# Layer 1's softmax in five later pieces: how the subtraction, the exponential and their maxima are placed among the score groups of an attention layer

## The chip, the core and the metric

The kernel runs on one core of a Trainium2 chip. The core has a matrix engine (PE, with its weight loads shown apart as PEld), a vector engine (DVE), a scalar engine (ACT), a general engine (POOL) and SyncE (SP), which issues most transfers. Each engine works through its own queue in order. Matrix results land in PSUM, a small memory that is cut into tiles here; everything else lies in SBUF or in device memory. The metric is the time of one execution in device microseconds; the kernel before took 3659.3 us, the median of three runs from 3655.91 to 3659.39.

## The reference

Four layers follow one another on a tensor of 4 images, 64 x 64 pixels and 128 channels, all in float32: layer 0 is neighbourhood attention with a gate, layer 1 is full attention over an image, layer 2 a gated mix with a layer norm, layer 3 a selective state-space scan. The change is in layer 1:

```python
N = H * W                                    # 4096
h = group_norm(x, gn_scale, gn_bias)
hf = h.reshape(B, N, C)
q = hf @ wq + bq
k = hf @ wk + bk
v = hf @ wv + bv
w_ = jnp.einsum('bqd,bkd->bqk', q, k) * C ** (-0.5)
w_ = jax.nn.softmax(w_, axis=2)
o = jnp.einsum('bqk,bkd->bqd', w_, v)
o = o @ wo + bo
return x + o.reshape(B, H, W, C)
```

Every pixel of an image attends to all 4096 pixels of it, so each image has a score matrix of 4096 x 4096.

## The kernel before

The images are worked on one after the other: layer 0 of an image, then its layer 1. While layer 1 runs, short tasks of other layers are put between its steps by a function `between(i)`: layer 2 of the same image (`turn`, `mix`, `add`, `norm`: transposes, products into PSUM tiles `pr`, `pg`, `pl`, `py`, layer-norm statistics) and the front of layer 3 (`front`: projections `pi` and `pz`, copies `xh`, a depthwise convolution whose taps are DVE, ACT and POOL work on `acc`, `tp` and `gsum`, and the products `pd`). The rest of layer 3 runs after the last image.

Layer 1 takes the queries in 16 blocks of 256 and the keys in 16 groups of 256 (two tiles of 128). Scores are held with keys on the partitions and queries along the free dimension, so that exponentials can serve directly as the stationary operand of the product with the values. One step `s` of the loop is one score group; `i, g = divmod(s, 16)` are its block and group. A step holds:

- `score` (L638 to L644): two products into one of four PSUM tiles `sc` (512 wide), a copy by ACT into `st` (L642), and a running maximum over groups by DVE into `mx` (L644). The tile is free again when copy and maximum have been made. After group 15, `fold` (L647) takes the maximum of the two halves of `mx`.
- At group 1 of the next block `turn_maxima` (L652 to L657): `mx` is transposed by PE (`pt`), a reduction by DVE gives each query's negated maximum `nm`, queries on the partitions, and two multiplications put it on the diagonal of a 128 x 256 tile `dm` (two identity matrices scaled by `nm`).
- At group 2 `soften` (L661 to L665): the product of a matrix of ones with `dm` spreads the negated maxima over all partitions into a PSUM tile `pb`; then, in four parts of four groups (2048 wide), DVE adds `pb` to `st` and ACT takes the exponential.
- `value` (L674): seven steps after that block's last score group, the groups of exponentials are multiplied into `po`, four products of 129 columns per group; column 128 of the values is one, so it yields the sum of the exponentials. Group `gv` of block `j` is due at step 16 (j + 1) + 7 + gv. After the last group `finish` divides by the sum (`ri`, L680) and adds the result to the image.

The exponentials of 24 groups have room in `st` (three buffers of eight groups). The PSUM tiles are handed out in turn from three pools: four tiles `s` for scores and for most products of the between-tasks, two tiles `t` for transposes, `pt`, `pb` and `pd`, two tiles `o` for `po`.

The order in which the loop writes these steps is not the order on the engines: when the program is built, a scheduler sets each engine's order by its own costs, except where an instruction is kept in program order. So the score groups and value groups of PE stand partly alternately and partly in runs.

ACT computes each kind of function with a table, and a change of kind needs a table load, a row of its own in the trace (ACT_TABLE_LOAD). Exponential, copy, identity and tanh need no change among each other here; Silu (L843) and Sqrt (L762) do.

The steps of the loop and where the between-tasks come in:

```python
if 0 < i <= NB and g == 1:
    turn_maxima(blocks[i - 1])
if 0 < i <= NB and g == 2:
    soften(i - 1, blocks[i - 1])
...
t = s // 8
if (s % 8 == 7 or s == ng * (NB + 1) + LAG - 1) and t > 0:
    between(t - 1)
```

So `between(0)` comes at step 15, the last group of the first block, and then one task at every eighth step. In the first image `between(0)` is empty; in the others it projects two chunks of the image before (four `pi`) and begins their convolution.

Of the kernel before, what the change touches and what calls it, by code (L numbers as in the profile page):

```python
# [23 lines left out]
AF = mybir.ActivationFunctionType  # L24
ALU = mybir.AluOpType
# [4 lines left out]
P = 128  # L30
# [108 lines left out]
def layers_0_to_2(  # L139
    ctx, tc, xf, mata, matb, rows, rpb, convw, sel, ident, cl, dram, big, ring, early, x3_d, ub_d, zf_d, y_d, dbl_d, ct_d, gw_d, bw_d  # L140
):
    nc = tc.nc
# [10 lines left out]
    def ps_t(shape, name):  # L153
        return psp.tile(shape, F32, name=name, tag="t", bufs=2)
# [31 lines left out]
    def load_x(b, xt=None, tiles=(0, NT), queue=nc.sync, kept=False):  # L186
        if xt is None:
            xt = ring([P, NT, C], f"x_{b}")
        src = xf[b].rearrange("(r w) c -> r w c", w=W)
        for j in range(*tiles):  # L190
            r, c = BR * (j // 4), BC * (j % 4)
            ins = queue.dma_start(xt[:, j, :], src[r:r + BR, c:c + BC, :])
            if kept:

                tc.keep_in_program_order(ins)
        return xt
# [19 lines left out]
    for cv, n in enumerate(cols_of):  # L216
        t = t_d[cv].rearrange("q h d k -> (q h) (d k)")
# [45 lines left out]
    ones = wp.tile([P, P], F32, name="ones")  # L263
# [64 lines left out]
    def edge_bias(rv):  # L328

        t = wp.tile([P, HEADS * 11 * 60], F32, name="be", tag="be")  # L330
        if rv in edge_d:
            nc.sync.dma_start(t, edge_d[rv])
        else:
            nc.gpsimd.memset(t, NEG)
            a = 0
            for cv in range(3):
                n = HEADS * 11 * cols_of[cv]
                fill_bias(t[:, a:a + n], rv, cv, 0 if rv == 0 else H - BR)
                a += n
            edge_d[rv] = dram.tile([P, HEADS * 11 * 60], F32, name=f"edge_d{rv}")  # L340
            nc.sync.dma_start(edge_d[rv], t)
        return t

    def bias_tiles():
        return [wp.tile([P, HEADS * 14 * n], F32, name=f"bias_m{k}", tag=f"bm{k}") for k, n in enumerate(cols_of)]
# [231 lines left out]
    def layer_1(b, xt, hT, st, between):  # L577
# [44 lines left out]
        QB, G, LAG, NB = 2 * P, 2, 7, L // (2 * P)  # L622
        ng = NT // G
# [5 lines left out]
        def group(s, n=1):  # L629
            r, at = divmod(s % (3 * 8), 8)  # L630
            return rings[r][:, G * at:G * (at + n), :]

        def score(i, k, g):
            if g == 0:
                k.mx = tmp.tile([P, G, QB], F32, name="mx1", tag="mx1")
            ps = ps_s([P, G, QB], "sc1")
            for r in range(G):
                nc.tensor.matmul(  # L638
                    ps[:, r, :], lhsT=kT[:, bass.ts(G * g + r, P)], rhs=qT[:, bass.ts(i, QB)], start=True, stop=True
                )  # L640
            st = group(ng * i + g)
            nc.scalar.copy(st, ps)  # L642
            if g > 0:
                nc.vector.tensor_tensor(k.mx, group(ng * i) if g == 1 else k.mx, ps, ALU.max)  # L644

        def fold(k):
            nc.vector.tensor_tensor(k.mx[:, 0, :], k.mx[:, 0, :], k.mx[:, 1, :], ALU.max)  # L647

        def turn_maxima(k):
            pt = ps_t([P, 2, P], "pt1")  # L650
            for h in range(2):
                nc.tensor.transpose(pt[:, h, :], k.mx[:, 0, bass.ts(h, P)], ident)  # L652
            nm = sml.tile([P, 2], F32, name="nm1", tag="nm1")
            nc.vector.tensor_reduce(nm, pt, AX.X, ALU.max, negate=True)
            k.dm = tmp.tile([P, 2, P], F32, name="dm1", tag="dm1", bufs=1)
            for h in range(2):
                nc.vector.tensor_scalar(k.dm[:, h, :], ident, nm[:, h:h + 1], None, ALU.mult)  # L657

        def soften(i, k):
            pb = ps_t([P, QB], "pb1")  # L660
            nc.tensor.matmul(pb, lhsT=ones, rhs=k.dm.rearrange("p h q -> p (h q)"), start=True, stop=True)  # L661
            for g in range(0, ng, 4):
                part = group(ng * i + g, 4)
                nc.vector.tensor_tensor(part, part, pb.unsqueeze(1).to_broadcast([P, 4 * G, QB]), ALU.add)  # L664
                nc.scalar.activation(part, part, AF.Exp)  # L665

        def value(i, k, g):
            if g == 0:
                k.po = ps_o([P, 2, C + 1], "po1")
            st = group(ng * i + g)  # L670
            for r in range(G):
                j = G * g + r
                for h in range(2):
                    nc.tensor.matmul(  # L674
                        k.po[:, h, :], lhsT=st[:, r, bass.ts(h, P)], rhs=v[:, j, :], start=(j == 0 and h == 0), stop=(j == NT - 1 and h == 1)
                    )

        def finish(i, k):
            ri = sml.tile([P, 2], F32, name="ri1", tag="ri1")
            nc.vector.reciprocal(ri, k.po[:, :, C])  # L680
            for h in range(2):
                x = xt[:, 2 * i + h, :]
                nc.vector.scalar_tensor_tensor(x, k.po[:, h, 0:C], ri[:, h:h + 1], x, ALU.mult, ALU.add)

        blocks = {}
        for s in range(ng * (NB + 1) + LAG):
            i, g = divmod(s, ng)
            if i < NB:
                k = blocks.setdefault(i, Block())
                score(i, k, g)  # L690
                if g == ng - 1:
                    fold(k)
            if 0 < i <= NB and g == 1:
                turn_maxima(blocks[i - 1])
            if 0 < i <= NB and g == 2:
                soften(i - 1, blocks[i - 1])
            j, gv = divmod(s - ng - LAG, ng)
            if j >= 0:
                value(j, blocks[j], gv)
                if gv == ng - 1:  # L700
                    finish(j, blocks.pop(j))
            t = s // 8
            if (s % 8 == 7 or s == ng * (NB + 1) + LAG - 1) and t > 0:
                between(t - 1)


# [440 lines left out]
    for b in range(B):  # L1147
# [8 lines left out]
        def between(i):  # L1156

            n, part = divmod(i - 6, 4)
            if i == 6 and b + 1 < B:
                ahead.append(load_x(b + 1))  # L1160
            if i >= 6 and n < NCH:
                parts[part](n)
            first_part(i)
            if b + 1 < B and i == NT + 1:
                edge_of[b + 1] = edge_bias(0)
            if b + 1 < B and i == NT + 3:
                bias_m[:] = bias_tiles()
                for t, d in zip(bias_m, bias_d):
                    nc.sync.dma_start(t, d)

        first_part = front(b)
        first_part(-1)
        layer_1(b, xt, *handed.pop(b), between)
        if b + 1 < B:
            coming = layer_0(b + 1, ahead[0], edge_of[b + 1])
# [385 lines left out]
```

## Time and profile before

| what | us |
|---|---|
| median of three runs | 3659.3 |
| the profiled execution | 3657.49 |
| its span on the engines | 3655.7 |
| layer 1, images 1 to 4, with the tasks between | 198 to 747, 918 to 1483, 1654 to 2218, 2388 to 2958 |
| layer 0 of images 1 to 4 | 0 to 198, 747 to 918, 1483 to 1654, 2218 to 2388 |
| layer 3's scans and output | about 3020 to 3656 |
| a score matmul start to start, a step's score group | 0.22, 0.87 |
| a value group of a step | 0.89 |
| addition of `pb`, 128 x 2048 (DVE, L664) | 2.28 |
| exponential, 128 x 2048 (ACT, L665) | 1.91 |
| score copy (ACT, L642) and maximum (DVE, L644), 128 x 512 | 0.59 and 0.69 |
| table load (ACT), 237 of them | 1.28 |

How to read it: PE shows two records for one float32 product, so a score group is four records and a value group eight. The idle time of a row is that of its engine just before it, and behind the arrow stands what ended it. In a windows line the numbers are the stretch, its length, the busy time of PE, PEld, DVE, ACT and POOL (with the number of instructions), the granted clock of PE as a share of full speed, the share of the transfer engines and GB/s.

### The profile page before, as it was taken

What the parts mean: (1) busy time and instruction counts of PE and PEld (TensorE: products, weight loads), DVE (VectorE), ACT (ScalarE), POOL (GpSimd) and SP (SyncE); (2) the same over time, 40 slices, a digit from 0 to 9 for tenths busy, and PEclk for the clock granted to TensorE, in tenths of its full rate; (3) what the DMA queues carried; (4) which work ended last, traced back from release to release, by engine and by line L of the source; (5) the groups of instructions that cost most, each with busy time, mean ns of one, the idle gap of its engine ahead of it and who ended that gap; (6) DMA issues with size and microseconds to landing.
All of it is one profiled execution on the core that took longest, in us unless ns stands there. A gap on an engine that the chain in (4) does not pass through costs nothing. (4 is left out here: it accounts for less than half of the span.)

```text
span 3655.7 us, 61448 instructions
## 1 busy us (share of the span) xinstructions
PE 3293.8 (90%) x22234; PEld 2603.0 (71%) x22234; DVE 2773.2 (76%) x5070; ACT 2619.3 (72%) x4324; POOL 1416.7 (39%) x1592
## 2 busy tenths in 40 slices
PE   7999999999999999998999999989999987666647
PEld 4679988866788888666888886668888852222246
DVE  5757777767768777677787776767877768999968
ACT  4855667778667777686676777866767759999934
POOL 6500012245112222451122224521222338999856
PEclk8999999999999999999999999999999995555579
DMA  4200000131001012410021213100100279999998
GB/s 123 73 25 3 12 18 27 54 100 35 24 27 45 27 45 87 135 39 24 24 79 30 77 54 101 40 1 24 45 30 34 69 225 211 214 238 217 201 275 284
DMA packets 189362, 310.38 MB, mean 85 GB/s; under 512 B 23007, under 2 KB 111996, under 8 KB 184156
## 3 DMA queue, kind: packets, MB, share of 16 engines
q1 hardware_dynamic: 146260, 220.27, 18.0%
q0 software_dynamic: 24384, 76.95, 11.9%
q10 hardware_dynamic: 18416, 9.24, 0.9%
q8 instruction: 176, 2.88, 0.3%
q14 instruction: 126, 1.03, 0.1%
HBM read 167.69 MB, written 155.56 MB: 88 GB/s over the span
## 5 line engine op out<-in xcount | busy, mean ns | idle before, releaser
L674 PEld LDWEIGHTS po<-v,st 128*128 128x128 f32 x8192 | 1049.2, 193 | 73.5 <-issue 35.7
L674 PE MATMUL po<-v,st 128*128 128x129 f32 x8192 | 1067.8, 277 | 17.6 <-ACT st L665 17.6
L638 PE MATMUL sc<-qT,kT 128*128 128x256 f32 x4096 | 1025.7, 382 | 12.7 <-DVE mx L644 12.5
L642 ACT COPY st<-sc 128x512 f32<-128x512 f32 x1024 | 580.5, 587 | 454.2 <-PE sc L638 452.6
L644 DVE TENSOR_TENSOR mx<-mx,sc 128x512 f32<-128x512 f32 x896 | 613.2, 684 | 275.7 <-ACT st L642 252.3
L638 PEld LDWEIGHTS sc<-qT,kT 128*128 128x128 f32 x4096 | 718.9, 191 | 105.7 <-issue 13.9
L664 DVE TENSOR_TENSOR st<-st,pb 128x2048 f32<-128x2048 f32 x256 | 572.4, 2280 | 29.0 <-PE pb L661 28.7
L665 ACT ACTIVATE st<-st 128x2048 f32<-128x2048 f32 x256 | 484.6, 1910 | 28.5 <-DVE st L664 27.2
L1271 PE MATMUL pdt<-dbl,dt 8*128 8x512 f32 x512 | 307.5, 1081 | 142.3 <-ACT de L1278 141.7
L1282 POOL TENSOR_TENSOR inp<-de,ub 128x1024 f32<-128x1024 f32 x128 | 409.6, 4391 | 6.8 <-ACT de L1278 6.3
L1271 PEld LDWEIGHTS pdt<-dbl,dt 8*128 8x128 f32 x512 | 114.2, 312 | 332.8 <-ACT de L1278 270.0
L505 POOL TENSOR_SCALAR pr<-pr,sm 128x308 f32<-128x308 f32 (+3 forms) x512 | 243.9, 496 | 205.1 <-DVE sm L503 186.8
L746 POOL TENSOR_TENSOR x<-x,row 128x512 f32<-128x512 f32 x32 | 47.9, 1498 | 707.1 <-DVE mx L644 686.7
L892 POOL TENSOR_TENSOR gsum<-gsum,tp 128x504 f32<-128x504 f32 (+1 forms) x177 | 229.2, 1301 | 127.1 <-ACT gsum L880 73.8
L497 ACT ACTIVATE pr<-pr,mx 128x308 f32<-128x308 f32 (+3 forms) x512 | 262.8, 517 | 1.3 <-DVE mx L486 1.3
L1309 DVE TENSOR_TENSOR_SCAN h<-h,end,inp 128x1024 f32<-128x1024 f32 x96 | 221.1, 2346 | 20.3 <-ACT h L1295 9.7
L514 PE MATMUL pt<-ident,pr 128*88 128x128 f32 (+5 forms) x1472 | 205.4, 276 | 9.8 <-ACT prT L516 8.8
L901 DVE SCALAR_TENSOR_TENSOR acc<-xh,cc,acc 128x512 f32<-128x512 f32 (+3 forms) x250 | 199.5, 803 | 10.2 <-ACT acc L865 8.6
L1324 POOL DMA_DIRECT2D y<-yo x112 | 200.6, 2710 | 13.1 <-DMA y<-y 4.8
L742 POOL TENSOR_TENSOR o<-o,rt 128x512 f32<-128x512 f32 x32 | 34.3, 1070 | 438.9 <-DVE o L741 434.4
L514 PEld LDWEIGHTS pt<-ident,pr 128*88 128x88 f32 (+5 forms) x1472 | 164.6, 138 | 45.2 <-ACT prT L516 25.9
L483 DVE CUSTOM_DVE_ANT_0 pr<-sc,bias_m 128x266 f32<-128x266 f32 (+1 forms) x384 | 152.1, 452 | 56.7 <-PE sc L479 55.1
(235 smaller groups left out, 4964.8 us busy)
## 6 DMA issues: line engine op xcount, KB each, us to landing
y<-yo POOLq DMA_DIRECT2D x112, 512.0 KB, 10.4
y<-y SPq DMA_DIRECT2D x48, 512.0 KB
zf_d<-zf SPq DMA_DIRECT2D x64, 256.0 KB
ub_d<-u SPq DMA_DIRECT2D x64, 256.0 KB
ub<-ub_d SPq DMA_DIRECT2D x16, 1024.0 KB
yl<-y SPq DMA_DIRECT2D x64, 256.0 KB
zc<-zf_d SPq DMA_DIRECT2D x64, 256.0 KB
v_d<-vg SPq DMA_DIRECT2D x128, 64.0 KB
```

The source lines that it names most:

```text
L497: pin(nc.scalar.activation(k.pr[:, h], k.pr[:, h], AF.Exp, bias=k.mx[:, h:h + 1], accum_out=k.sm[:, h:h + 1]))
L505: nc.gpsimd.tensor_scalar(k.pr[:, h], k.pr[:, h], k.sm[:, h:h + 1], 1.0, ALU.mult, ALU.mult)
L514: pin(nc.tensor.transpose(pt[0:n, h, :], k.pr[:, h, at:at + n], ident))
L638: nc.tensor.matmul(ps[:, r, :], lhsT=kT[:, bass.ts(G * g + r, P)], rhs=qT[:, bass.ts(i, QB)], start=True, stop=True)
L642: nc.scalar.copy(st, ps)
L644: nc.vector.tensor_tensor(k.mx, group(ng * i) if g == 1 else k.mx, ps, ALU.max)
L664: nc.vector.tensor_tensor(part, part, pb.unsqueeze(1).to_broadcast([P, 4 * G, QB]), ALU.add)
L665: nc.scalar.activation(part, part, AF.Exp)
L674: nc.tensor.matmul(k.po[:, h, :], lhsT=st[:, r, bass.ts(h, P)], rhs=v[:, j, :], start=(j == 0 and h == 0), stop=(j == NT - 1 and h == 1))
L892: nc.gpsimd.tensor_tensor(a, a, p, ALU.add)
L1271: nc.tensor.matmul(pdt[j][:, g, :], lhsT=dt[o:o + RANK, P * f:P * f + P], rhs=at(dbl[o:o + RANK, :], k & 2, g0, g0 + CH), start=True, stop ...
L1282: nc.gpsimd.tensor_tensor(by_rows(inp), by_rows(de), at(ub_s[f], b ^ (k & 1), SC * n, SC * n + SC), ALU.mult)
```

## The change

Three things are rewritten, and the computation stays the same. The two multiplications for the diagonal become one tensor_tensor of the identity and the negated maxima, both broadcast. The product with ones moves from group 2 to group 3 (`spread`). The subtraction and the exponential are no longer made in one go of four parts but in five parts at groups 3, 4, 5, 7 and 9, the first two of them two groups wide (1024) and the others four. Besides, the first task between the steps, `between(0)`, moves from step 15 to step 20, group 4 of the second block; all other tasks stay.

```diff
             k.dm = tmp.tile([P, 2, P], F32, name="dm1", tag="dm1", bufs=1)
-            for h in range(2):
-                nc.vector.tensor_scalar(k.dm[:, h, :], ident, nm[:, h:h + 1], None, ALU.mult)
-
-        def soften(i, k):
-            pb = ps_t([P, QB], "pb1")
-            nc.tensor.matmul(pb, lhsT=ones, rhs=k.dm.rearrange("p h q -> p (h q)"), start=True, stop=True)
-            for g in range(0, ng, 4):
-                part = group(ng * i + g, 4)
-                nc.vector.tensor_tensor(part, part, pb.unsqueeze(1).to_broadcast([P, 4 * G, QB]), ALU.add)
-                nc.scalar.activation(part, part, AF.Exp)
+            nc.vector.tensor_tensor(
+                k.dm, ident.unsqueeze(1).to_broadcast([P, 2, P]), nm.unsqueeze(2).to_broadcast([P, 2, P]), ALU.mult
+            )
+
+        def spread(k):
+            k.pb = ps_t([P, QB], "pb1")
+            nc.tensor.matmul(k.pb, lhsT=ones, rhs=k.dm.rearrange("p h q -> p (h q)"), start=True, stop=True)
+
+        softened = {3: (0, 2), 4: (2, 2), 5: (4, 4), 7: (8, 4), 9: (12, 4)}
+
+        def soften(i, k, g, n):
+            part = group(ng * i + g, n)
+            nc.vector.tensor_tensor(part, part, k.pb.unsqueeze(1).to_broadcast([P, n * G, QB]), ALU.add)
+            nc.scalar.activation(part, part, AF.Exp)
...
-            if 0 < i <= NB and g == 2:
-                soften(i - 1, blocks[i - 1])
+            if 0 < i <= NB and g == 3:
+                spread(blocks[i - 1])
+            if 0 < i <= NB and g in softened:
+                soften(i - 1, blocks[i - 1], *softened[g])
...
             t = s // 8
-            if (s % 8 == 7 or s == ng * (NB + 1) + LAG - 1) and t > 0:
+            if s == ng + 4:
+                between(0)
+            elif (s % 8 == 7 or s == ng * (NB + 1) + LAG - 1) and t > 1:
                 between(t - 1)
```

## The prediction

> **What bounds the kernel now.** I read the page's busy shares and slices first, then the stages by windows, then the idle time of TensorE by group inside layer 1, and last the timeline at one place. The page:
>
> ```profile
> PE 3293.8 (90%) x22234; PEld 2603.0 (71%) x22234; DVE 2773.2 (76%) x5070; ACT 2619.3 (72%) x4324; POOL 1416.7 (39%) x1592
> ...
> PE   7999999999999999998999999989999987666647
> ...
> PEclk8999999999999999999999999999999995555579
> ...
> L664 DVE TENSOR_TENSOR st<-st,pb 128x2048 f32<-128x2048 f32 x256 | 572.4, 2280 | 29.0 <-PE pb L661 28.7
> L665 ACT ACTIVATE st<-st 128x2048 f32<-128x2048 f32 x256 | 484.6, 1910 | 28.5 <-DVE st L664 27.2
> ```
>
> TensorE is full in the first 33 slices; layer 3 behind them is another regime, which the change doesn't touch. Layer 1 of the four images, from first score to last value product (window, its length, then busy PE, PEld, DVE, ACT, POOL, then the granted clock):
>
> ```profile
> 221.80:747.00 525.20, 512.40 (x3382) 463.44 (x3381) 398.57 (x575) 345.33 (x442) 68.84 (x59) 0.99 0.08 26
> 941.30:1483.00 541.70, 527.62 (x3475) 467.88 (x3474) 417.12 (x603) 389.74 (x519) 126.62 (x112) 0.99 0.15 45
> 1678.00:2218.00 540.00, 525.87 (x3467) 466.11 (x3466) 418.37 (x603) 389.30 (x518) 128.38 (x113) 0.99 0.17 52
> 2412.00:2957.20 545.20, 532.09 (x3478) 468.55 (x3477) 423.44 (x611) 399.86 (x536) 145.81 (x136) 0.99 0.14 44
> ```
>
> PE is busy 98%; it idles 12.8, 14.1, 14.1 and 13.1 us, 54.1 in all. DVE has over 120 us to spare per image and ACT over 140. The 54.1 us are the ceiling, with what the clock loses after an idle stretch. All of the idle time stands before three groups (second image):
>
> ```profile
> L674 PE MATMUL po<-v,st 128*128 128x129 f32 x2048 | 266.6, 276 | 4.8 <-ACT st L665 4.8
> L638 PE MATMUL sc<-qT,kT 128*128 128x256 f32 x1024 | 257.0, 382 | 3.3 <-DVE mx L644 3.2
> ...
> L661 PE MATMUL pb<-dm,ones 128*128 128x256 f32 x32 | 10.5, 409 | 6.0 <-DVE dm L657 5.3 <-DVE rd L763 0.4
> ```
>
> In the same view images 1, 3 and 4 give 3.1, 4.8, 4.8 (po), 4.0, 3.3, 2.1 (sc) and 5.6, 6.0, 6.1 (pb). Sums over four images: po 17.5, sc 12.7, pb 23.7. The timeline where the second image's first values begin:
>
> ```profile
> 965.21 0.70 PE L661 MATMUL pb<-dm,ones 128*128 128x256 f32 x2 [1.52 <-DVE dm L657]
> 965.75 1.89 PE L638 MATMUL sc<-qT,kT 128*128 128x256 f32 x8
> 972.46 4.64 PE L674 MATMUL po<-v,st 128*128 128x129 f32 x20 [4.83 <-ACT st L665]
> ...
> 966.74 8.87 DVE L664 TENSOR_TENSOR st<-st,pb 128x2048 f32<-128x2048 f32 x4
> ...
> 969.12 1.28 ACT L665 ACT_TABLE_LOAD   x1
> 970.41 7.31 ACT L665 ACTIVATE st<-st 128x2048 f32<-128x2048 f32 x4
> ```
>
> PE runs out of scores and waits for a whole 2048-wide subtraction and exponential. DVE takes no maximum for 8.87 us, so the score buffers stay full. Then the clock falls:
>
> ```profile
> 972.40:978.40 6.00, 5.94 (x24) 5.70 (x25) 5.79 (x7) 5.32 (x3) 0.29 (x1) 0.50 0.00 0
> ```
>
> 6 us at 0.50 lose 3.0 us. The same windows at the other starts: 1705.5 to 1712.3 and 2439.4 to 2446.2 at 0.50 with 4.5 and 4.8 us of work (2.25 and 2.4 lost), 247.4 to 252 at 0.63 (1.7 lost); and twice in mid-image 1, 504 to 507.4 and 562 to 565.4 at 0.50 (1.7 each). Together 12.75, so the ceiling is 54.1 + 12.75 = 66.9 us.
>
> **Part by part.** A step is one score group (0.87 us of PE by the starts) and one value group (0.89), 1.76 us.
>
> *Five parts; layer 2/3 work moved at the start.* From the 512-wide maximum (686 ns) and the 2048-wide addition (2280) I interpolate 1.22 us for a 1024-wide addition; a 1024-wide activation takes 1.06 (u, L843). So the first values can begin 2.28 + 1.91 - 1.22 - 1.06 = 1.9 us sooner after pb. In images 2 to 4 `between(0)` also moves (in image 1 it is empty). It issues no DMA; with it POOL's row copies and ACT's first convolution products come five steps later, 3 steps ahead of the next task, which needs them. Its four projections `pi`, which stood before pt, now stand around pb, by the order of the built program: scores 0 to 4, one pi, pb, three pi, score 5, po. Counted from the last score of block 1, pb stands at five groups x 0.87 + pt 0.22 + one pi 0.86 = 5.4; then PE has pb 0.5, three pi 2.6 and a score group 0.9, and wants po at 9.4. ACT evicts the first pi (to 6.2), does acc 0.81, tp 0.72, the load 1.28 and the half-size exponential 1.06: 10.1. PE waits 0.7 instead of 4.83, and pb doesn't wait. Now gone: po 17.5, the pb waits there (1.52, 1.52, 1.17 = 4.2) and the half clock behind (9.35), 31.0. I leave 1.0 per image for this wait and scores that wait for pi's buffers: 27.0 saved. Bounds: 8 (1.9 x 4) and 31. I take near the upper, since what fills the gap are products that have to run anyway.
>
> *pb a group later.* Between pt and pb stood one step of PE work, 1.76 us, in nearly all blocks; in the built program it is 3.3 to 3.5. The other pb waits, 23.7 - 4.2 = 19.5, are at most 2.5 long, one such per image; 1.76 more cover leaves about 0.65 x 4 = 2.6: 16.9 saved, bounds 0 and 19.5. What is queued behind the longer-held result: pb keeps one of two "t" buffers until the fifth addition, at about group 10; the next products that need that buffer come with the tasks of group 15, so nothing waits. New is that the fourth addition stands on DVE behind ri, which waits for the last value product of the block before (group 6); its values are wanted at group 15, and behind it only maxima could be late.
>
> *The diagonal by one product.* Two of 0.28 become one 256-wide tensor_tensor; the nearest row is the fold, 424 ns. -0.1 to +0.15 us, off the path with 1.76 us of new cover: 0. It no longer has a maximum between its halves, which in the 2.5 us waits stood waiting for a score copy.
>
> *Bursts broken up.* Additions stand three in a row (6.67 us) or four between two maxima; in the built program mostly one, at worst a 1024 and a 2048 (3.4, eased by four score buffers x 1.76 us). Of sc's 12.7 I leave 3.0, and the two half-clock stretches of image 1 go (3.4), since the 2.0 and 2.5 us waits ahead of them do: 13.1 saved, bounds 0 and 16.1.
>
> *What is added.* Per block one addition (2 x 1.22 - 2.28 = 0.16) and one exponential (2 x 1.06 - 1.91 = 0.21); and with exponentials spread over groups 3 to 9, other tables come between: 266 loads stand in ACT's order instead of 237. 29 x 1.28 = 37 us plus 64 x 0.21 = 13: 50 us of ACT, 13 per image, against 140 us spare. Nothing on the path if scores are copied in time. Where a part with its load stands between two copies of even blocks, ACT goes 6.7 us without a copy (sg, o 0.69 each, exponential 1.91, load 1.28, zf 1.08, u 1.06) against 4.8 before; PE comes back to a buffer after 3 x 1.76 + 0.89 = 6.2 us. Bounds 0 and 1.0 us x 28 such places; I take 4, because the four matmuls pg, pl, pz that stand there give PE 3.4 us more.
>
> [...] ACT's row above has the exponential start at 970.41, right behind a load of 1.28 from 969.12, with no drain between them. [...]
>
> [...]
>
> **Sum.** 27.0 + 16.9 + 13.1 - 4 = 53.0 us. The profiled execution took 3657.5 (span 3655.7), 1.8 under the median 3659.3; I take the sum off the median: 3606.
>
> **Rivals.**
> 1. *Only the start gains.* In even blocks the order now puts three more convolution taps (0.73 each) between the fold of the maxima and their turning, 5.6 us of DVE work instead of 3.2, because additions took their earlier places. 2.4 more work against 1.76 more cover: pb waits 0.64 us longer in some 28 blocks, 18 us, which eats the 16.9; if DVE's maxima lag alike, the 13.1 too. Time 3659 - 27 + 4 = 3636. Against it: DVE idles before maxima for 65 us per image (waits for score copies), so the moved taps find room.
> 2. *Slower.* ACT at group 7 of the even blocks, with the 6.7 us above: if its exponential also waits there for the fourth addition, scores stall. Each us lost costs 28; without the 4 us that I allowed the gain is 57, so from 57 / 28 = 2.0 us per place it is gone, and at 3 us the time is 3659 - 57 + 84 = 3686. Against it: by the rows the fourth addition ends about 11 us after pb, just as ACT has finished o; a stall needs DVE some 2 us later.
> 3. *No change.* The scheduler's order had already filled the gaps with long runs of value products, and only the places of the waits move: 3659. Against it: the built order now alternates scores and values almost throughout, and the start has new work in its gap.
> 4. *All of it.* The ceiling goes, and with it delays that the idle time hides: a score matmul counts as busy 0.38 us but starts every 0.22, so up to 0.16 us before each of 64 pb: 3659 - 67 - 10 = 3582. Against it: the same order must then suit every block.
>
> **How the numbers follow.** Forecast 0.59 (3592 to 3622), only the start 0.16, all of it 0.10, no change 0.05, slower 0.10. The range leaves out no change, slower and half of "all of it": 3585 to 3641, which is the start alone plus 5. Measurement tells about 0.2% (7 us) from no change: faster 0.85, same 0.05, slower 0.10.
>
> **What would show it.** Right: po's idle before the first values under 1 us per image, with no half-clock window behind; pb's idle under 1.5 us per image; sc's near 1; layer-1 windows about 13 us shorter each; loads 266; 64 more additions and exponentials. Wrong: PE idle before sc released by ACT st or DVE mx in even blocks at groups 8 to 11 (rival 2), or pb's idle unchanged with taps ahead of nm (rival 1). What would make it wrong is one in-order queue: a maximum or copy standing behind an instruction that waits.

## The result and the profile after

The changed kernel takes 3664.65 us (median of 22 runs, 3659.95 to 3668.65) against 3657.12 us for the kernel before (22 runs, 3652.32 to 3663.18): a ratio of 1.0021, 95% interval 1.0015 to 1.0027. That is 7.5 us slower where 53 us faster was forecast. The profiled execution has a span of 3663.1 us.

The page of the changed kernel, its busy shares, TensorE's slices and the groups that answer to those shown of before:

```profile
PE 3285.4 (90%) x22234; PEld 2595.9 (71%) x22234; DVE 2856.5 (78%) x5070; ACT 2664.0 (73%) x4417; POOL 1430.2 (39%) x1592
...
PE   7999999999999999999999999999999887666647
...
L638 PE MATMUL sc<-qT,kT 128*128 128x256 f32 x4096 | 1045.9, 382 | 50.4 <-DVE mx L644 50.2
L678 PE MATMUL po<-v,st 128*128 128x129 f32 x8192 | 1070.1, 275 | 2.2 <-ACT st L669 2.2
...
L668 DVE TENSOR_TENSOR st<-st,pb 128x2048 f32<-128x2048 f32 (+1 forms) x320 | 589.2, 1852 | 24.5 <-PE pb L662 24.5
```

The row of the product with ones, from the groups view:

```profile
L662 PE MATMUL pb<-dm,ones 128*128 128x256 f32 x128 | 38.9, 386 | 7.2 <-DVE dm L656 6.4 <-ACT st L642 0.7
```

TensorE's idle time before value products fell from 17.6 to 2.2 us. Its idle time before scores, released by a maximum on VectorE, rose from 12.7 to 50.4 us. VectorE is busy 83 us longer (2773.2 to 2856.5); the additions account for 17 of these (572.4 to 589.2), and no new kind of work was added.

Layer 1 of the four images in windows, first score to last value product (length, busy PE, PEld, DVE, ACT, POOL, granted clock):

```profile
221.20:734.70 513.50, 506.94 (x3381) 458.81 (x3381) 400.31 (x575) 350.64 (x462) 70.74 (x59) 1.00 0.08 27
930.80:1476.40 545.60, 526.10 (x3469) 465.99 (x3469) 443.56 (x603) 401.83 (x543) 131.44 (x112) 1.00 0.15 46
1671.20:2215.80 544.60, 525.78 (x3469) 465.86 (x3469) 442.83 (x603) 401.71 (x543) 132.75 (x113) 1.00 0.17 52
2410.00:2964.90 554.90, 533.52 (x3482) 469.48 (x3481) 456.12 (x612) 414.08 (x562) 147.98 (x136) 0.99 0.13 43
```

Image 1 became 11.7 us shorter (525.2 to 513.5), close to the 13 forecast. Images 2 to 4 became 3.9, 4.6 and 9.7 us longer; the sum is +6.5 us, most of the loss (the two spans differ by 7.4). TensorE's idle time in these windows rose from 54.1 to 66.3 us; its busy time fell by 5.6, with the granted clock at 1.00 instead of 0.99 in images 1 to 3. Image 1 differs in POOL: 71 us of work in its window against 131 to 148 in the others. In images 2 to 4 DVE's busy time rose by 26, 24 and 33 us for the same number of instructions (603, 603, and 612 against 611).

Which instructions grew is seen tile by tile (minimum, median and maximum in ns). The changed kernel:

```profile
L778 DVE TENSOR_SCALAR x<-x,mv,rd x128: 333/350/8290, 353.0 to 2993.8; 128x128 f32<-128x128 f32 x128
```

The kernel before:

```profile
L770 DVE TENSOR_SCALAR x<-x,mv,rd x128: 328/342/1433, 358.2 to 2984.8; 128x128 f32<-128x128 f32 x128
```

This is the normalisation of layer 2, a task that stands between layer 1's steps and that the diff doesn't touch. Its 128 instructions, summed one by one, went from 63.8 to 123.9 us. The convolution taps on DVE (`acc`) went from 200.8 to 233.4 us. The timeline at one place that both programs have, the end of the fourth image, shows why. Before:

```profile
2903.04 1.77 POOL L985 DMA_DIRECT2D y<-du  x2
...
2904.08 0.68 DVE L644 TENSOR_TENSOR mx<-mx,sc 128x512 f32<-128x512 f32 x1
...
2904.20 3.16 POOL L993 TENSOR_TENSOR u<-u,bb 128x512 f32<-128x512 f32 x2
...
2904.68 6.67 DVE L664 TENSOR_TENSOR st<-st,pb 128x2048 f32<-128x2048 f32 x3
...
2906.68 3.12 POOL L892 TENSOR_TENSOR gsum<-gsum,tp 128x504 f32<-128x504 f32 x2
...
2909.13 1.90 POOL L895 TENSOR_TENSOR acc<-acc,gsum 128x512 f32<-128x512 f32 x1
```

After:

```profile
2902.35 1.76 POOL L993 DMA_DIRECT2D y<-du  x2
...
2903.26 9.62 DVE L778 TENSOR_SCALAR x<-x,mv,rd 128x128 f32<-128x128 f32 x2
...
2903.51 3.13 POOL L1001 TENSOR_TENSOR u<-u,bb 128x512 f32<-128x512 f32 x2
...
2905.97 3.07 POOL L900 TENSOR_TENSOR gsum<-gsum,tp 128x504 f32<-128x504 f32 x2
...
2908.39 1.86 POOL L903 TENSOR_TENSOR acc<-acc,gsum 128x512 f32<-128x512 f32 x1
2909.61 1.84 POOL L900 TENSOR_TENSOR gsum<-gsum,tp 128x504 f32<-128x504 f32 x1
2911.53 1.26 POOL L903 TENSOR_TENSOR acc<-acc,gsum 128x512 f32<-128x512 f32 x1
...
2913.53 2.07 PE L638 MATMUL sc<-qT,kT 128*128 128x256 f32 x4 [6.35 <-DVE mx L644]
```

POOL does the same work in both, and the transfer engines are about equally busy (share 0.96 before and 1.00 after, from 2903 to 2913 us). Before, a burst of three additions stands beside it on DVE and takes its usual 6.67 us. After, the burst is gone from there, two normalisations stand in its place, and they need 9.62 us (two of them take 0.60 us at 2900.5 in the kernel before): they end at 2912.88, when POOL's chain ends (2912.79). No maximum is taken meanwhile, the four score buffers are full, and PE waits 6.35 us. From 2909.5 on, while it still waits, the clock is down, as the windows view shows:

```profile
2909.50:2916.40 6.90, 2.87 (x9) 2.50 (x10) 6.90 (x7) 1.56 (x3) 3.22 (x3) 0.51 0.97 319
```

I counted DVE's instructions up to 3020 us by whether more than 30% of their length lay beside a POOL product or copy:

| DVE instruction | clear of POOL | beside POOL, before | beside POOL, after |
|---|---|---|---|
| normalisation `x`, both operands and result in SBUF | 0.34 us | 1.06 us (28 of 128) | 1.56 us (66 of 128) |
| tap `acc`, two tensors from SBUF | 0.73 us | 1.10 us (48 of 250) | 1.37 us (80 of 250) |
| addition, 2048 wide, one operand in PSUM | 2.28 us | 2.28 us (76 of 256) | (two widths mixed) |
| maximum `mx`, one operand in PSUM | 0.68 us | 0.68 us (55 of 896) | 0.68 us (64 of 896) |

The two kinds with an operand in PSUM aren't slowed (2.28 and 0.68 us beside POOL as clear of it); the other two are: the normalisation from 0.34 us to 1.06 and 1.56, the tap from 0.73 to 1.10 and 1.37. The prediction priced neither as depending on what stands beside it. The runs show only who is slowed and beside whom; what in the core makes it so, none of them shows.

Of the waits of `sc` over 0.15 us, 50.2 us in all, 48.8 us stand where a normalisation longer than 1 us ended within the 12 us before, all in odd blocks at groups 6 to 9 (counted from the order of the score products, blocks from 0). Only 15.6 us of them (groups 6 and 7) come with the stretched instruction or just behind it. In the other 33.2 us (groups 8 and 9) PE waits for a maximum that stands behind additions: there VectorE works off what it is behind. That the normalisation is what put it behind is shown by the experiments, not by this count.

### The profile page after: what moved, and what is told of

It is laid out like the page before. It is cut to its first block, busy times and chain, and to the rows that moved or that the text cites. A ratio compares the mean times of both kernels' runs of the same rounds, so it can differ in the third digit from the quotient of the medians.

```text
span 3663.1 us, 61358 instructions
## 1 busy us (share of the span) xinstructions
PE 3285.4 (90%) x22234; PEld 2595.9 (71%) x22234; DVE 2856.5 (78%) x5070; ACT 2664.0 (73%) x4417; POOL 1430.2 (39%) x1592
## 4 chain that ended last, share of the span: by engine, by line
PE 50%; DVE 19%; issue 10%; ACT 10%; POOL 6%; DMA 4%; SPq 0%; ACTq 0%; DVEq 0%; POOLq 0%
PE po L678 15%; PE sc L638 15%; DVE mx L644 4%; PE pt L514 4%; DVE acc L909 3%; POOL inp L1290 3%; PE sc L479 3%; DVE st L668 2%; PE po L525 2%; POOL y L1332 2%; DVE x L778 2%; DVE h L1317 1%; ACT st L669 1%; ACT st L642 1%; PE pp L535 1%
## 5 line engine op out<-in xcount | busy, mean ns | idle before, releaser
L638 PE MATMUL sc<-qT,kT 128*128 128x256 f32 x4096 | 1045.9, 382 | 50.4 <-DVE mx L644 50.2
L638 PEld LDWEIGHTS sc<-qT,kT 128*128 128x128 f32 x4096 | 710.0, 191 | 140.4 <-DVE mx L644 60.5
L669 ACT ACTIVATE st<-st 128x2048 f32<-128x2048 f32 (+1 forms) x320 | 501.6, 1569 | 151.0 <-DVE st L668 148.2
L668 DVE TENSOR_TENSOR st<-st,pb 128x2048 f32<-128x2048 f32 (+1 forms) x320 | 589.2, 1852 | 24.5 <-PE pb L662 24.5
L900 POOL TENSOR_TENSOR gsum<-gsum,tp 128x504 f32<-128x504 f32 (+1 forms) x177 | 243.2, 1380 | 160.7 <-ACT gsum L888 100.3
L909 DVE SCALAR_TENSOR_TENSOR acc<-xh,cc,acc 128x512 f32<-128x512 f32 (+3 forms) x250 | 232.2, 934 | 9.2 <-ACT acc L873 7.8
L516 ACT COPY prT<-pt 110x512 f32<-110x512 f32 (+3 forms) x240 | 139.0, 579 | 69.3 <-PE pt L514 68.9
```

The source lines that it names most:

```text
L638: nc.tensor.matmul(ps[:, r, :], lhsT=kT[:, bass.ts(G * g + r, P)], rhs=qT[:, bass.ts(i, QB)], start=True, stop=True)
L668: nc.vector.tensor_tensor(part, part, k.pb.unsqueeze(1).to_broadcast([P, n * G, QB]), ALU.add)
L909: nc.vector.scalar_tensor_tensor(acc, x, c, acc, ALU.mult, ALU.add)
```

## The experiments

**Theory A:** the loss is VectorE beside GpSimd. The additions, which GpSimd doesn't disturb (2.28 us beside it as clear of it), have left the places beside GpSimd's products, and the normalisation and the taps have come to stand there. **Theory B:** the loss is the new order itself: taps ahead of the maxima's turn, pieces of additions between maxima, more table loads; GpSimd has no part in it. Changes below are medians against the kernel before on the same chip (3658.0 to 3658.8 us). Expectations give the normalisation as a sum of its instructions.

### The task moved alone

```diff
-            if (s % 8 == 7 or s == ng * (NB + 1) + LAG - 1) and t > 0:
+            if s == ng + 4:
+                between(0)
+            elif (s % 8 == 7 or s == ng * (NB + 1) + LAG - 1) and t > 1:
                 between(t - 1)
```

> The kernel before with one part of the change alone: the tasks of the first call between(0) move from step 15 to step 20 of an image; the additions stay one burst at group 2. Theory A (the loss of the whole change is VectorE beside GpSimd: the normalisation of layer 2 and the taps of the convolution now stand next to GpSimd's products): the burst stays where it is, so the normalisation stays near its 63.8 us of busy time and the taps near 200.8, and the start of images two to four keeps what the first term of my sum gave it without the wait for pb, about 17.5 us of waits for po and 9 us of half clock less 4 given back: some 20 us below the kernel before, near 3637. Theory B (the loss is the new order itself: taps ahead of the maxima's turn, pieces of additions between maxima, more table loads): none of these is in this kernel, so the same 3637. Both fall if it is within 5 us of the kernel before: then the start was never worth anything.

Measured: 3641.26 us, ratio 0.9953 (0.9941 to 0.9966), 17.2 us faster. The groups view of this kernel:

```profile
L674 PE MATMUL po<-v,st 128*128 128x129 f32 x8192 | 1061.2, 276 | 5.5 <-ACT st L665 5.5
L638 PE MATMUL sc<-qT,kT 128*128 128x256 f32 x4096 | 1024.9, 382 | 13.6 <-DVE mx L644 13.4
```

The waits for `po` fell from 17.6 to 5.5 us, `sc` stayed, and so did the normalisation. The first step of the change does what was forecast, at about two thirds of the size (image 1, where the moved call is empty, still waits 3.1 us for `po`), and it is the only one of the three that keeps the old places of the additions.

### The product with ones and the burst a group later, alone

```diff
-            if 0 < i <= NB and g == 2:
+            if 0 < i <= NB and g == 3:
                 soften(i - 1, blocks[i - 1])
```

> The kernel before with the product with ones and its burst of four additions and exponentials moved from group 2 to group 3, nothing else. Theory A: the additions stay one burst of 9.1 us, which lies beside GpSimd's products as before, so the normalisation stays below 75 us of busy time and the taps below 210, and the waits for pb (8 to 8.6 us an image) go: 15 to 20 us below the kernel before, near 3640. Theory B: the taps now stand between the fold and nm in half of the blocks (4.0 us of VectorE instead of 3.2) and cover less than the product needs: the waits for pb stay in these blocks, the waits of sc for mx grow by more than 10 us, and the time is within 8 us of the kernel before or above it.

Measured: 3657.56 us, ratio 1.0001 (0.9991 to 1.0012). The waits of PE in layer 1 (in total, times, longest) and the normalisation:

```profile
PE sc L638 <- DVE mx L644: 24.1, 12, 4.3
...
PE pb L661 <- DVE dm L657: 7.9, 8, 1.8
```

```profile
L770 DVE TENSOR_SCALAR x<-x,mv,rd x128: 333/345/4920, 358.4 to 2984.1; 128x128 f32<-128x128 f32 x128
```

Theory A's number fell, theory B's came true, but not by B's mechanism: the waits for `pb` did go (21.7 to 7.9 us), so the taps ahead of nm were covered. What took the gain is +11.6 us of waits of `sc` for `mx`, all behind normalisations, whose sum rose from 63.8 to 89.7 us. The burst was kept whole but moved one group, and one group was enough to leave GpSimd's products uncovered: 76 of the 256 additions lay beside GpSimd before, 41 here, and of the normalisations 28 and 48. Counted in time up to 2990 us, the additions lay beside GpSimd's products and copies for 132.6 us before and for 77.1 here. A was wrong to think that a burst covers wherever it stands.

### The changed kernel with the task back in its old place

```diff
-            if s == ng + 4:
-                between(0)
-            elif (s % 8 == 7 or s == ng * (NB + 1) + LAG - 1) and t > 1:
+            if (s % 8 == 7 or s == ng * (NB + 1) + LAG - 1) and t > 0:
                 between(t - 1)
```

> The changed kernel with the first call between(0) put back at step 15. Theories A and B alike: the waits for po at the start of images two to four come back (4.8 us each and the half clock behind them), 15 to 22 us above the changed kernel, 3680 to 3687; the normalisation stays above 110 us of busy time and the waits of sc for mx near 50 us. If instead the place of between(0) is what brought VectorE's work beside GpSimd's, the normalisation falls to 75 us or less and the time to 3655 or below.

Measured: 3662.80 us, ratio 1.0009 (1.0000 to 1.0018), like the changed kernel. A miss for both theories: the waits for `po` didn't come back (0.0 us in its groups view). The timeline at the second image's first values:

```profile
953.51 0.70 PE L662 MATMUL pb<-dm,ones 128*128 128x256 f32 x2 [1.53 <-DVE dm L656]
...
957.59 1.10 PE L638 MATMUL sc<-qT,kT 128*128 128x256 f32 x4 [0.69 <-DVE mx L644]
959.22 0.70 PE L638 MATMUL sc<-qT,kT 128*128 128x256 f32 x2 [0.54 <-DVE mx L644]
959.76 1.95 PE L678 MATMUL po<-v,st 128*128 128x129 f32 x16
```

With half-size first pieces the first values are ready when PE has finished its scores; 2.8 us of waits for `pb` and `mx` remain where 6.4 stood. In the full change the moved task and the small pieces remove the same wait, and one would do. The normalisation stays long (114.8 us busy), so the task's place isn't what brought it beside GpSimd.

### The changed kernel with its five parts in one row

```diff
-            if 0 < i <= NB and g in softened:
-                soften(i - 1, blocks[i - 1], *softened[g])
+            if 0 < i <= NB and g == 3:
+                for part in softened.values():
+                    soften(i - 1, blocks[i - 1], *part)
```

> The changed kernel with all five parts of the additions and exponentials at group 3, in a row behind the product with ones: the burst is back, a group later, and everything else of the change stays. Theory A: the burst covers GpSimd's products again, so the normalisation falls from 123.9 us to below 80, the taps from 233.4 to below 212, the waits of sc for mx from 50 us to below 25, and the time to 3615 to 3630. Theory B: the taps ahead of nm stay and the row of additions between two maxima is longer (9.2 us instead of 3.4): waits of sc at or above 50 us, time at 3660 or above.

Measured: 3638.18 us, ratio 0.9943 (0.9929 to 0.9956): 20.3 us faster than before, 27.8 us faster than the full change (20.3 + 7.5). Its waits and its normalisation:

```profile
PE sc L638 <- DVE mx L644: 33.6, 22, 5.0
```

```profile
L779 DVE TENSOR_SCALAR x<-x,mv,rd x128: 333/346/8548, 354.8 to 2967.6; 128x128 f32<-128x128 f32 x128
```

The direction is A's, the size is half: the normalisation sums to 99.0 us, not under 80, and 33.6 us of waits are left. A's reason isn't borne out either: the row did not come back beside GpSimd's products, where the additions now lie for 61.3 us (55.3 in the full change, 132.6 before). Fewer normalisations and taps lie there (67.8 and 65.7 us, against 95.9 and 93.7 in the full change); why this order does that, no run isolates. B is refuted in its second part: the longer row of additions did not make waits longer. The split, which was to save 13.1 us, costs 27.8.

### GpSimd's product left out, in both kernels

```diff
-                engine.tensor_tensor(u, u, bb, ALU.mult)
+                if engine is not None:
+                    engine.tensor_tensor(u, u, bb, ALU.mult)
...
-                    times_b(*c, x_of.pop((*c, "b")), nc.gpsimd)
+                    times_b(*c, x_of.pop((*c, "b")), None)
```

Changed kernel:

> The changed kernel without GpSimd's product of u with B in layer 2 (this multiplication of the reference is left out; all else is computed). It removes about 1.0 us times 128 of GpSimd's work beside VectorE and nothing from VectorE or TensorE. Theory A: the normalisation, whose longest instructions lie beside this product and the one for gsum, falls from 123.9 us of busy time to 60 to 85, the waits of sc for mx from 50 us to 30 or less, and the time by 15 to 35 us, to 3630 to 3650. Theory B: the order on VectorE is the same, so sc waits stay near 50 us and the time within 5 us of the changed kernel.

Kernel before:

> The kernel before without GpSimd's product of u with B in layer 2 (this multiplication of the reference is left out; all else is computed). The partner of the same edit of the changed kernel. Theory A: the product lay beside the burst of additions, so the normalisation falls only from 63.8 us to about 45 to 55, and the time by 0 to 8 us, to 3649 to 3657; the changed kernel without the product is below this one. Theory B: the two edits change the two kernels alike, and the changed one stays some 7 us above this one.

Measured: the changed kernel falls to 3623.22 us (ratio to before 0.9908, 0.9895 to 0.9922); the kernel before doesn't move: 3657.56 us (0.9995, 0.9987 to 1.0004). The changed kernel without the product, groups view and then the normalisation:

```profile
L638 PE MATMUL sc<-qT,kT 128*128 128x256 f32 x4096 | 1043.2, 381 | 18.2 <-DVE mx L644 17.3
```

```profile
L778 DVE TENSOR_SCALAR x<-x,mv,rd x128: 333/343/2826, 355.5 to 2950.4; 128x128 f32<-128x128 f32 x128
```

The edit takes 48 instructions of 1.47 us from an engine that is busy 39% of the time; my expectation counted them wrongly as 128 of 1.0. In the changed kernel that is worth 43 us (7.5 + 35.6), in the kernel before nothing that can be told from none. An order on VectorE that costs by itself can't do this: B falls. The normalisation's sum falls by 39 us (123.9 to 84.6) and the waits of `sc` by 32. The sizes miss: the changed kernel falls below the 3630 to 3650 expected, and in the kernel before the normalisation stays at 61.0 us, where 45 to 55 was expected.

### The normalisation on ScalarE, in both kernels

```diff
+            nb = sml.tile([P, 4], F32, name="nb2", tag="nb2")
+            nc.vector.scalar_tensor_tensor(nb, mv[:, :, 0], -1.0, rd, ALU.mult, ALU.mult)
             for k in range(4):
                 x = xt[:, 4 * n + k, :]
-                nc.vector.tensor_scalar(x, x, mv[:, k, 0:1], rd[:, k:k + 1], ALU.subtract, ALU.mult)
+                nc.scalar.activation(x, x, AF.Identity, bias=nb[:, k:k + 1], scale=rd[:, k:k + 1])
```

Changed kernel:

> The changed kernel with the normalisation of layer 2, x = (x - m) * rd, on ScalarE as an Identity with scale rd and bias -m * rd (one small VectorE instruction per tile makes the bias); everything is computed. It takes 123.9 us from VectorE and puts 128 instructions of 0.3 to 0.4 us on ScalarE, about 45 us. Theory A: the instructions that stretched to 2 to 8 us beside GpSimd are gone from VectorE's row, sc waits for mx fall from 50 us to 25 or less and the time by 20 to 40 us, to 3625 to 3645. Theory B: VectorE loses only the 44 us that these instructions take when clear, little of it on the path: within 8 us of the changed kernel. Against both: ScalarE becomes late with the exponentials, pt waits for st, and the time rises.

Kernel before:

> The kernel before with the normalisation of layer 2 on ScalarE in the same way; everything is computed. Theory A: of its 63.8 us on VectorE only some 20 were beside GpSimd, so the gain is at most 5 to 10 us, 3647 to 3660, and smaller than the gain of the same edit in the changed kernel. Theory B: the same difference in both kernels.

Measured: the changed kernel 3611.61 us (0.9871, 0.9856 to 0.9886), the kernel before 3650.19 us (0.9976, 0.9968 to 0.9985). The same edit is worth 54.7 us in the one (7.5 + 47.2) and 8.6 us in the other. The changed kernel with it:

```profile
L638 PE MATMUL sc<-qT,kT 128*128 128x256 f32 x4096 | 1041.7, 381 | 1.6 <-DVE mx L644 1.4
L911 DVE SCALAR_TENSOR_TENSOR acc<-xh,cc,acc 128x512 f32<-128x512 f32 (+3 forms) x250 | 233.2, 938 | 8.0 <-ACT acc L875 6.4
L780 ACT ACTIVATE x<-x,nb,rd 128x128 f32<-128x128 f32 x128 | 56.2, 488 | 30.0 <-DVE nb L777 30.0
```

The waits of `sc` are gone (50.4 to 1.6 us), more than expected, and the time is below the 3625 to 3645 expected. The taps are as slow as in the changed kernel (233 us) and cost little: 1.1 us of the waits of `sc` stand behind a tap. Of the two stretched kinds, it was mostly the normalisation that stood where maxima were due. It takes 0.49 us each on ACT, where 0.3 to 0.4 was expected.

### Two combinations with it

The two edits above that need no new code: the five parts in one row with the normalisation on ScalarE, and the kernel before with the task moved and the normalisation on ScalarE.

```diff
+                nc.scalar.activation(x, x, AF.Identity, bias=nb[:, k:k + 1], scale=rd[:, k:k + 1])
...
+                for part in softened.values():
+                    soften(i - 1, blocks[i - 1], *part)
```

> The changed kernel with its five parts in one row at group 3 and the normalisation of layer 2 on ScalarE; everything is computed. It prices the split of the burst alone once the normalisation no longer stands beside GpSimd: the split kernel with the same normalisation took 3611.6 us. My forecast's own term for the split (13.1 us: waits of sc for mx 12.7 to 3.0 us and a half clock of 3.4) makes this one 3625. If the waits of sc were only ever the normalisation beside GpSimd, a burst without it waits no more than the pieces, as the kernel before with this edit showed (0.6 us), and this one is at 3605 to 3614: then the split is worth nothing and its 26 table loads and smaller parts are a small loss.

```diff
+            if s == ng + 4:
+                between(0)
...
+                nc.scalar.activation(x, x, AF.Identity, bias=nb[:, k:k + 1], scale=rd[:, k:k + 1])
```

> The kernel before with the first call between(0) at step 20 and the normalisation on ScalarE; everything is computed. The two gains lie in different places (start of an image; waits of sc), so they should add: 3658.5 less 17.2 less 8.6, 3632 to 3634. The difference to the changed kernel with the normalisation on ScalarE (3611.6) is then the worth of the product with ones and the additions a group later, about 21 us, near the 16.9 us that my forecast put on it.

Measured: 3608.22 us (0.9862, 0.9849 to 0.9876), as expected where the split is worth nothing, and 3628.67 us (0.9920, 0.9907 to 0.9932), below the 3632 to 3634 expected. With what stands above, the change can be priced step by step, with the normalisation on VectorE and off it (difference to the kernel before on the same chip):

| | normalisation on DVE | step | on ACT | step |
|---|---|---|---|---|
| order of before | 0 | | -8.6 | |
| task moved | -17.2 | -17.2 | -29.4 | -20.8 |
| and product with ones later, diagonal by one product, five parts in one row | -20.3 | -3.1 | -49.8 | -20.4 |
| and the parts spread (the full change) | +7.5 | +27.8 | -47.2 | +2.6 |

Off VectorE the steps add as the prediction thought, apart from the split, which is worth nothing or costs a little: the intervals of the last two kernels overlap. The row of parts still makes PE wait for `sc`, 7.9 us against 1.6 with the pieces:

```profile
L638 PE MATMUL sc<-qT,kT 128*128 128x256 f32 x4096 | 1019.5, 381 | 7.9 <-DVE mx L644 7.8
```

But the pieces wait 6.2 us for `pb` against 2.0, and nothing of the difference reaches the time. With the normalisation on VectorE the second and the third step lose 17 and 25 us against that.

### The normalisation on GpSimd

```diff
-                nc.vector.tensor_scalar(x, x, mv[:, k, 0:1], rd[:, k:k + 1], ALU.subtract, ALU.mult)
+                nc.gpsimd.tensor_scalar(x, x, mv[:, k, 0:1], rd[:, k:k + 1], ALU.subtract, ALU.mult)
```

> The changed kernel with the normalisation of layer 2 on GpSimd instead of VectorE, same instruction, all computed. GpSimd can't hold itself off: it runs these 128 instructions in its own queue behind its products. If the loss is that VectorE stands still while GpSimd works, VectorE's maxima are free again: sc waits for mx fall from 50 us to 20 or less and the time to 3612 to 3635, although GpSimd now has 40 to 80 us more work, and the taps on VectorE beside it may grow past 233 us. If the loss is only that the normalisation is late for its readers, it is later still here: pt waits for x grow by tens of us and the time rises above 3664.

Measured: 3602.48 us, ratio 0.9853 (0.9838 to 0.9868), below the 3612 to 3635 expected and the fastest kernel of this study: 55.6 us below before, 63 below the changed kernel, by one word. Its tile view and its waits:

```profile
L778 POOL TENSOR_SCALAR x<-x,mv,rd x128: 778/793/1286, 354.4 to 2931.3; 128x128 f32<-128x128 f32 x128
```

```profile
PE pt L297 <- POOL x L778: 13.1, 12, 3.3
...
PE sc L638 <- DVE mx L644: 2.1, 5, 0.6
```

GpSimd takes 0.79 us for what VectorE does in 0.34, and its readers wait a little longer (`pt` 10.4 to 13.1 us). The normalisation's own lateness was never the loss; that VectorE stood still with it was.

### The diagonal by two instructions again

```diff
-            nc.vector.tensor_tensor(
-                k.dm, ident.unsqueeze(1).to_broadcast([P, 2, P]), nm.unsqueeze(2).to_broadcast([P, 2, P]), ALU.mult
-            )
+            for h in range(2):
+                nc.vector.tensor_scalar(k.dm[:, h, :], ident, nm[:, h:h + 1], None, ALU.mult)
```

> The changed kernel with the diagonal of the maxima by two tensor_scalar instructions again. Forecast's term: nothing, so within 6 us of the changed kernel (3658 to 3670). Rival: the one product reads two operands of SBUF and is held beside GpSimd (0.74 us there, 0.42 clear); then this one is 5 to 15 us faster and GpSimd's products for gsum fall from 243 us towards 229.

Measured: 3672.94 us, ratio 1.0041 (1.0028 to 1.0054), about 7 us slower than the changed kernel. Both expectations miss. The one product saves: `dm` takes 40.8 us in the changed kernel and this here, with the wait of `pb` behind it at 15.5 us instead of 7.2:

```profile
L657 DVE TENSOR_SCALAR dm<-ident,nm 128x128 f32<-128x128 f32 x128 | 59.2, 500 | 0.4
L661 PE MATMUL pb<-dm,ones 128*128 128x256 f32 x128 | 40.5, 398 | 15.5 <-DVE dm L657 13.7 <-ACT st L642 1.8
```

Clear of GpSimd the two take 0.28 us each and the one 0.42; beside it 0.62 each and 0.74. Two held instructions cost more than one, which is the likely reason; no run here takes GpSimd away from beside them.

## Why the prediction was wrong

*The start of each image: right in kind, about a third too large.* `po` waits 2.2 us in all, and the half clock at the starts is gone (granted 1.00 from 244 to 252, 954 to 962, 1680 to 1720 and 2425 to 2455 us): at the second image's first values

```profile
954.80 1.80 PE L678 MATMUL po<-v,st 128*128 128x129 f32 x14 [0.72 <-ACT st L669]
```

stands where 4.83 stood; the working had 0.7. The 27.0 us measure 17 to 21 with the task moved alone. The sum also took image 1's 3.1 us of `po` and 1.7 us of half clock as filled, where the moved call is empty; with the task alone the 3.1 us stay (the clock there isn't shown), and in the full change, with its smaller first pieces, both are gone. That the pieces would bring the gain without the moved task, the sum didn't see: its lower bound gave them 8 us.

*The product with ones a group later: the wait was right, the time wasn't.* `pb` fell from 23.7 to 7.2 us, 1.0 to 2.7 per image. Off VectorE's conflict the step gives about 20 us with the diagonal and the row of parts (16.9 forecast). With the normalisation on VectorE it gives 0 to 3.

*The bursts broken up: this is the step that failed.* It counted 13.1 us saved, bounds 0 and 16.1. The waits of `sc` that it let fall from 12.7 to 3.0 us rose to 50.4, and the step costs 27.8 us. What it had wrong is the cost of a row of additions, and that nothing else would change its length: with the pieces 66 instead of 28 of the 128 normalisations lay beside GpSimd's products, and VectorE fell behind there. The 12.7 us do end behind additions, as I read them, but 11.2 us stand where a normalisation longer than 1 us had ended within the 12 us before, and with the normalisation on ScalarE and the additions still in a row 0.6 us are left: the row alone was not their cause. In the changed kernel without the conflict the row costs 7.9 us of `sc` waits, and breaking it up still saves no time (+2.6 us). Even in image 1, with little GpSimd work, these waits didn't fall (4.0 to 5.0 us). The half clock in mid-image 1 did go, as the term had it (granted 1.00 from 480 to 600 us).

*Its hidden assumption.* Every term priced VectorE's instructions at their means in the trace of before, and said that VectorE has over 120 us to spare per image. It still has 102 in the second image. The normalisation's row stood in the trace of before with a median of 342 and a maximum of 1433 ns; a spread of four in an instruction of fixed shape was a sign that its length depends on its neighbours (0.34 us clear of POOL, 1.06 beside it), and the change moves neighbours. I looked for what waits on a semaphore, and this waits on none: the stretch is booked as busy time.

*What is added:* 266 loads as forecast, ACT up 45 us against 50 estimated, and the 1024-wide addition takes the 1.21 us that was interpolated. None of it is on the path: the rival that had ACT stall at group 7 found no `sc` wait on ACT. Of my signs for "wrong", PE idle before `sc` released by DVE's maximum did show, at groups 6 to 9 of odd blocks and from another cause. *Only the start gains* had moved convolution taps as its reason; taps and fold were covered, as `pb` shows. *The diagonal*, costed at nothing, is a gain of 7 us.

With the normalisation on ScalarE the change is worth 38.6 us (47.2 less the 8.6 that this edit brings alone), some three quarters of the 53 forecast. The missing 14 us are the split (13.1 forecast, 2.6 lost) and the start's excess (27.0 against 20.8), less the 4.0 that was allowed for and 3.5 that the product with ones gave over its 16.9.

## What to carry to other kernels

Before moving work on VectorE, list which of its instructions have all operands in SBUF and what GpSimd does at the places where they will stand; the two kinds with an operand in PSUM kept their length beside GpSimd here (2.28 and 0.68 us), the other two went from 0.34 to 1.56 and from 0.73 to 1.37 us in the changed kernel. A long run of these may be what keeps the others out of harm's way, which is only suggested: from before over the burst a group later to the full change, the additions' time beside GpSimd falls (132.6, 77.1, 55.3 us) as the normalisation's sum rises (63.8, 89.7, 123.9). Read minimum, median and maximum of a row, not its mean: here a spread at fixed shape (342 ns in the median, 1433 at most) was a conflict already being paid for, booked as busy time, and reordering made it grow or shrink. Where two engines conflict, try giving the short instruction to the engine that it conflicts with, even at over twice its length (0.79 us against 0.34), or to a third (0.49): both paid here (55.6 and 47.2 us below before).

## What the runs showed of the hardware

- In the changed kernel two DVE normalisations that take 0.34 us each clear of GpSimd took 9.62 us beside a chain of seven GpSimd products, and ended with the last of them (2912.88 and 2912.79). The longest single one took 8.29 us, and in the kernel with the diagonal by two instructions 8.94.
- 48 GpSimd products of 1.47 us were worth 43 us of time in the changed kernel's order of VectorE and nothing that can be told from none in that of before.
- In the changed kernel PE's wait of 6.35 us for a maximum behind these normalisations (2907.2 to 2913.5) runs into a stretch of 6.9 us from 2909.5 at a granted clock of 0.51, in which PE has 2.87 us of work; by estimate that work would be some 1.4 us shorter at full clock (2.87 x 0.49).
